# One pipeline, two planners: scheduling the main loop of a two-layer kernel as a block of its own

## The chip, the cores and the metric

The kernel runs on one core of a Trainium2 chip. A core has five engines that each work through their own stream of instructions: TensorE (PE in the profile, with its weight loads as PEld), VectorE (DVE), ScalarE (ACT), GpSimd (POOL) and SyncE (SP), which here only issues DMAs. The streams run beside one another and meet at semaphores. The metric is the device time of one execution in microseconds, the median of three runs.

## The reference

The input is x, 16 sequences of 512 tokens with 256 channels. Two layers are applied, each an attention part and a feed-forward part. Each part first normalises x over the channels, scales and shifts it by values that come from a small condition vector (`mods` in the kernel), and its output is multiplied by a gate from the same condition and added to x.

- Layer 0, attention: q, k and v are projections of the input, passed through a short causal convolution over four tokens and SiLU. Sixteen heads of width 16 then run a recurrence over chunks of 16 tokens. Per head there are two fast weights of 4 x 16, W_in and W_out. For every chunk the softmax of k and of q against W_in over the four rows gives hidden values; they make the output of the chunk and an update of W_out; then W_in and W_out are updated twice by small attentions over the chunk's k and v. A layer norm over each head, an output gate and a projection follow.
- Layer 0, feed-forward: a low-rank network, 256 to 64 to 1024, GELU, back to 64 and to 256.
- Layer 1, attention: sixteen heads, causal, over a window of 64 tokens and the first four tokens of the sequence.
- Layer 1, feed-forward: a channel mix with the token before, `sigmoid(r) * (relu(k)^2 @ W_v)`.

All of it is in 32-bit floating point, apart from masks and some exact helpers in bf16.

## The kernel before

**Units.** The work is cut into 16 units (NU). A unit is 64 tokens (TB) of 8 sequences (HB); the 16 sequences are two halves, and even and odd units belong to the two halves. Layer 0's recurrence carries its state from one unit of a half to the next one of that half, in a bank of PSUM (`fws`).

**Streams.** Five generator functions each do one stage of a unit and yield now and then: `prepare` (normalisation, the projections and convolutions, SiLU at the end of each of q, k and v; results are written to DRAM), `chain` (two pieces of 32 tokens, each two calls of `recur`, the recurrence over 16 tokens, and `finish_piece`), `mlp` (output projection of layer 0's attention, then `low_rank_ffn`), `attend` (`window_attention`) and `mix` (`channel_mix`).

**The order in which it is traced.** `timetable(u)` gives each stream of unit u a number of steps and the times, counted in units, at which they are due: `prepare` from u-1.7, `chain` from u to u+2, `mlp` from u+2, `attend` from u+2.65, `mix` from u+4.1 to u+4.7. The last lines of `adaln_blocks` sort all steps by these times and advance each generator by one step. So instructions of several units and stages are traced interleaved, and the two halves' recurrences run beside each other.

**The order on the engines.** The order of tracing is not the order of issue. The framework takes the traced program with its data dependencies, gives each instruction a priority by its place in the trace, and plays the program through in a simulator: whenever an engine can take an instruction, the ready one of the best priority is put next in that engine's stream. On-chip buffers are assigned at the same time, by what is free in the simulated time. The streams that result are fixed; the chip then executes each in order and waits where the data isn't there. In the kernel before, this simulator is the framework's ordinary core simulator. `tc.high_priority()` raises what is traced under it (the GELU matmuls at line 728 and the bursts of `run`), and `run` (lines 212 to 227) pins a burst of activations that share a table behind one another and then loads the table with Exp and Ln back. The loads that are needed between two activations with different tables are put in afterwards.

**Lines to follow.** In the recurrence: the outer products on POOL (line 526), the scores and sums on DVE (lines 519, 520, 628), the scan on DVE (line 623), exponentials on ACT (line 534). In the window attention: all small matmuls go through one helper at line 865, for scores with queries as rows (`sc`), scores with keys as rows (`st`), scores against the first tokens (`tg`), values (`py`) and sums (`pz`); the masks are added by a matmul at line 862; ACT makes the exponentials `pT` (line 918) and `pg` (line 929) and the reciprocal of the sums `rs` (lines 967, 968); DVE multiplies (`yT`, line 972). In the channel mix: `mix` is made by ACT (line 1021) and DVE (line 1022) in one buffer that is used twice per unit, `pka` (line 1031) is the matmul that reads it, `ka` (line 1043) its relu. Table loads carry lines 217 and 227 where `run` makes them. SP issues every DMA; `load_gate` (line 374) loads a gate into a ring of one buffer per stream.

**Buffers.** PSUM has three rotating banks for projections (`bank`), four for attention scores and the feed-forward (`abank`), and one for the recurrence. The setup ahead of the pipeline (weights, masks, the modulation values and gates) is traced first; its scratch pool is closed before the pools of the pipeline are opened.

Of the kernel before, what the change touches and what calls it, by code (L numbers as in the profile page):

```python
# [95 lines left out]
def adaln_blocks(ctx: ExitStack, tc: tile.TileContext, a: dict, out: bass.AP):  # L96
# [1023 lines left out]
    steps = []  # L1120
    for u in range(NU):
        for n, (f, parts) in enumerate(timetable(u)):
            times = [s + (e - s) * (k + 0.5) / count for count, s, e in parts for k in range(count)]
            stream = f(u)
            steps += [(t, n, k == len(times) - 1, stream) for k, t in enumerate(times)]
    for _, _, last, stream in sorted(steps, key=lambda s: s[:2]):
        next(stream, None)
        if last:
            assert next(stream, steps) is steps


# [52 lines left out]
```

## Time and profile before

| | before |
|---|---|
| median of 3 runs | 3306.56 us (3290.19 to 3310.29) |
| the profiled execution | 3303.97 us, span 3302.2 us |
| granted clock of TensorE, mean | 0.78 |
| busy: PE, DVE | 73%, 73% |
| busy: ACT, POOL | 53%, 51% |
| weight loads of PE | 44% |
| DMA | 186.42 MB, mean 56 GB/s |
| instructions | 46348 |

The profile is one execution. Busy shares are per engine over the span; the forty slices show a digit per fortieth of it (9 is 90% or more); the chain that ended last is followed back from the last instruction, at each step to what released it. Rows of waits name the waiting engine, tile and line, then what released it, then the total, the count and the longest. In rows of the timeline, the bracket is the engine's idle time before the row and its releaser. In the tables of stretches the granted clock is a share of TensorE's full clock.

### The profile page before, as it was taken

What the parts mean: (1) busy time and instruction counts of PE and PEld (TensorE: products, weight loads), DVE (VectorE), ACT (ScalarE), POOL (GpSimd) and SP (SyncE); (2) the same over time, 40 slices, a digit from 0 to 9 for tenths busy, and PEclk for the clock granted to TensorE, in tenths of its full rate; (3) what the DMA queues carried; (4) which work ended last, traced back from release to release, by engine and by line L of the source; (5) the groups of instructions that cost most, each with busy time, mean ns of one, the idle gap of its engine ahead of it and who ended that gap; (6) DMA issues with size and microseconds to landing.
All of it is one profiled execution on the core that took longest, in us unless ns stands there. A gap on an engine that the chain in (4) does not pass through costs nothing.

```text
span 3302.2 us, 46348 instructions
## 1 busy us (share of the span) xinstructions
PE 2424.1 (73%) x16784; PEld 1461.5 (44%) x16784; DVE 2396.2 (73%) x4513; ACT 1762.1 (53%) x3738; POOL 1669.3 (51%) x1575
## 2 busy tenths in 40 slices
PE   3541255777787878788887878788797878878886
PEld 2210123444444445454554445454454455545564
DVE  1678787868887787788778877877878877774221
ACT  1662354556655656565655656565665645444443
POOL 0245555556566655545546555555556556543112
PEclk7675576878787877878778788788878786869887
DMA  5321112032314131231304122131403121212010
GB/s 149 78 62 19 45 40 67 24 72 56 81 33 96 30 83 46 59 78 43 81 21 100 30 70 67 43 88 37 91 17 95 28 71 34 59 35 58 15 29 27
DMA packets 439305, 186.42 MB, mean 56 GB/s; under 512 B 323937, under 2 KB 413090, under 8 KB 439074
## 3 DMA queue, kind: packets, MB, share of 16 engines
q1 hardware_dynamic: 439074, 183.44, 22.8%
q8 instruction: 132, 2.16, 0.3%
q14 instruction: 99, 0.81, 0.1%
HBM read 116.66 MB, written 66.72 MB: 56 GB/s over the span
## 4 chain that ended last, share of the span: by engine, by line
DVE 32%; PE 28%; POOL 18%; ACT 11%; issue 7%; DMA 3%; SPq 1%; POOLq 0%; DVEq 0%; ACTq 0%
POOL pd_o L526 4%; POOL pd_i L526 4%; DVE pd_kv L623 4%; DVE pp L452 3%; DVE sc_v L519 3%; PE ph L728 3%; PE py L865 3%; PE st L865 2%; PE pz L865 2%; DVE sv L520 2%; PE pproj L994 2%; POOL pd_kv L526 2%; DVE mx L881 2%; DVE do L628 2%; PE pka L1031 2%
## 5 line engine op out<-in xcount | busy, mean ns | idle before, releaser
L526 POOL TENSOR_TENSOR pd_o<-e_k,dt_v 128x1024 f32<-128x1024 f32 x128 | 299.0, 2343 | 234.4 <-DVE e_k L541 234.2
L865 PE MATMUL st<-qs,keys 32*128 32x128 f32 x2048 | 234.3, 351 | 107.2 <-DVE mx L881 47.8
L526 POOL TENSOR_TENSOR pd_i<-e_v,dt_k 128x1024 f32<-128x1024 f32 x128 | 297.3, 2354 | 21.4 <-DVE e_v L541 21.1
L865 PEld LDWEIGHTS st<-qs,keys 32*128 32x128 f32 x2048 | 199.5, 240 | 163.0 <-DVE mx L881 61.5
L653 POOL TENSOR_TENSOR pd_kv<-hid,pd_kv 128x1024 f32<-128x1024 f32 x64 | 150.7, 2354 | 188.8 <-DVE fw L624 183.1
L628 DVE TENSOR_REDUCE do<-pd_o 128x64 f32<-128x1024 f32 x126 | 152.5, 1214 | 100.3 <-POOL pd_o L526 100.3
L628 DVE TENSOR_REDUCE di<-pd_i 128x64 f32<-128x1024 f32 x128 | 155.3, 1213 | 85.7 <-POOL pd_i L526 85.7
L865 PE MATMUL sc<-keys,qs 32*128 32x128 f32 x2048 | 169.5, 321 | 63.0 <-DVE mx L881 43.4
L700 PE MATMUL pwo<-w_WoT,oT 128*128 128x256 f32 x256 | 103.1, 560 | 142.6 <-POOL oT L693 140.7
L865 PEld LDWEIGHTS sc<-keys,qs 32*128 32x128 f32 x2048 | 134.6, 210 | 129.8 <-DVE mx L881 63.4
L881 DVE TENSOR_REDUCE mx<-sc 128x4 f32<-128x512 f32 x256 | 168.4, 679 | 19.0 <-PE sc L862 19.0
L623 DVE TENSOR_TENSOR_SCAN pd_kv<-within,pd_kv 128x1024 f32<-128x1024 bf16 x64 | 176.5, 2758 | 1.0
L526 POOL TENSOR_TENSOR pd_kv<-hid,dt_v 128x1024 f32<-128x1024 f32 x64 | 150.1, 2345 | 45.9 <-DVE hid L615 41.0
L519 DVE TENSOR_TENSOR sc_k<-tok,fw 128x1024 f32<-128x1024 f32 x128 | 155.5, 1215 | 16.0 <-ACT tok L589 14.6
L994 PE MATMUL pproj<-w_proj,yT 128*128 128x256 f32 x512 | 136.7, 411 | 36.7 <-DVE yT L972 33.7
L217 ACT ACT_TABLE_LOAD x110 | 141.1, 1283 | 19.7 <-PE pQ L735 18.1
L519 DVE TENSOR_TENSOR sc_v<-tok,fw 128x1024 f32<-128x1024 f32 x128 | 150.4, 1215 | 1.4
L865 PE MATMUL py<-pT,values 128*32 128x128 f32 x2048 | 130.4, 374 | 26.8 <-ACT pT L918 26.3
L520 DVE TENSOR_REDUCE sv<-sc_v 128x64 f32<-128x1024 f32 x128 | 149.7, 1210 | 0.0
L972 DVE TENSOR_TENSOR yT<-py,rs 128x256 f32<-128x256 f32 x128 | 51.5, 415 | 133.8 <-ACT rs L968 133.7
L918 ACT ACTIVATE pT<-st 128x512 f32<-128x512 f32 x256 | 135.4, 615 | 22.0 <-PE st L862 21.8
L865 PE MATMUL py<-pg,vglob 32*32 32x128 f32 x1536 | 71.8, 342 | 99.1 <-ACT pg L929 99.1
(244 smaller groups left out, 6821.5 us busy)
## 6 DMA issues: line engine op xcount, KB each, us to landing
values<-values SPq DMA_DIRECT2D x56, 256.0 KB
gate_a<-gates SPq DMA_DIRECT2D x64, 128.0 KB
xa<-in_x_dram SPq DMA_DIRECT2D x32, 256.0 KB
x<-in_x_dram SPq DMA_DIRECT2D x32, 256.0 KB
gate_c<-gates SPq DMA_DIRECT2D x64, 128.0 KB
gate_d<-gates SPq DMA_DIRECT2D x64, 128.0 KB
q<-y SPq DMA_DIRECT2D x64, 128.0 KB
dt_q<-q SPq DMA_DIRECT2D x32, 256.0 KB
```

Of the source, the lines that this page charges most:

```text
L217: ins = nc.scalar.activation(*args[0], **args[1])
L519: engine.tensor_tensor(pr, tok.unsqueeze(1).to_broadcast(every), w.unsqueeze(2).to_broadcast(every), mul)
L520: nc.vector.tensor_reduce(dst, pr, AX.X, add)
L526: engine.tensor_tensor(pr, hid.unsqueeze(2).to_broadcast(every), tok.unsqueeze(1).to_broadcast(every), mul)
L623: nc.vector.tensor_tensor_scan(flat, within, flat, 0.0, mul, add)
L628: nc.vector.tensor_reduce(t, pr, AX.X, add)
L653: nc.gpsimd.tensor_tensor(po, qh.unsqueeze(2).to_broadcast([P, R, D, CH]), upto, mul)
L700: nc.tensor.matmul(po[:, n * C : (n + 1) * C], lhsT=pair(oT, k, 2 * b2 + n), rhs=w_o[:, k, :], start=k == 0, stop=k == 1,)
L865: nc.tensor.matmul(dst, lhsT=lhsT, rhs=rhs, start=start, stop=False, skip_group_check=True)
L881: nc.vector.tensor_reduce(mx[:, j], sc[j].rearrange("p (s k) -> p s k", s=NS), AX.X, ALU.max)
L918: nc.scalar.activation(pT[j], st[j], AF.Exp)
L994: nc.tensor.matmul(po[:, n * C : (n + 1) * C], lhsT=yT[:, k2, par].rearrange("p e t -> p (e t)"), rhs=w_proj[:, k2, par, :], start=k2 == 0 ...
```

## The change

The loop that advances the generators is put in a `with` block. `tc.block` traces what is inside as a block of its own: it is always entered, and the planner treats it as one piece that is not mixed with what stands outside (here the setup; nothing follows). With `schedule_with_timeline_sim=True` the order inside is made with the framework's timeline model, which keeps track of each engine's sequencer, its execution and its queues apart, in place of the core simulator. The traced instructions, their order of tracing, their engines and their priorities relative to one another stay as they are.

```diff
             stream = f(u)
             steps += [(t, n, k == len(times) - 1, stream) for k, t in enumerate(times)]
-    for _, _, last, stream in sorted(steps, key=lambda s: s[:2]):
-        next(stream, None)
-        if last:
-            assert next(stream, steps) is steps
+    with tc.block(schedule_with_timeline_sim=True):
+        for _, _, last, stream in sorted(steps, key=lambda s: s[:2]):
+            next(stream, None)
+            if last:
+                assert next(stream, steps) is steps
```

## The prediction

> **What bounds the kernel now.** I read the page first: busy shares, the forty slices, the chain that ended last.
>
> ```profile
> span 3302.2 us, 46348 instructions
> PE 2424.1 (73%) x16784; PEld 1461.5 (44%) x16784; DVE 2396.2 (73%) x4513; ACT 1762.1 (53%) x3738; POOL 1669.3 (51%) x1575
> ...
> PE   3541255777787878788887878788797878878886
> ...
> DVE  1678787868887787788778877877878877774221
> ...
> DVE 32%; PE 28%; POOL 18%; ACT 11%; issue 7%; DMA 3%; SPq 1%; POOLq 0%; DVEq 0%; ACTq 0%
> ```
>
> No engine is full, and the chain changes engine all the time: this is a pipeline in which TensorE and VectorE are about equally loaded, and what is lost is lost in hand-overs. So I cut the span into stretches. The scan of line 623 comes back in the chain at 1751.21 and at 2499.59 us, four units apart, so a unit takes 187.1 us in the steady part. The table of stretches has for one such unit, for the end, and (from a second call) for the middle of that unit in steps of 4 us:
>
> ```profile
> 1939.00:2126.00 187.00, 151.98 (x1110) 91.51 (x1106) 150.41 (x280) 110.38 (x234) 102.38 (x98) 0.81 0.24 60
> ...
> 2970.00:3100.00 130.00, 111.45 (x1066) 71.98 (x1066) 47.83 (x103) 66.33 (x137) 43.56 (x54) 0.88 0.16 41
> ...
> 2064.00:2068.00 4.00, 0.00 (x0) 0.00 (x0) 3.93 (x8) 2.70 (x6) 1.89 (x3) 0.85 0.00 0
> 2068.00:2072.00 4.00, 3.94 (x38) 2.17 (x38) 1.88 (x2) 2.98 (x5) 4.00 (x3) 0.50 0.00 0
> 2072.00:2076.00 4.00, 4.00 (x34) 1.51 (x32) 3.83 (x8) 3.10 (x6) 1.36 (x1) 0.50 0.00 0
> 2076.00:2080.00 4.00, 4.00 (x45) 2.32 (x47) 3.86 (x6) 2.83 (x3) 0.00 (x0) 0.50 0.00 0
> 2080.00:2084.00 4.00, 4.00 (x25) 1.32 (x18) 3.65 (x10) 2.49 (x5) 2.95 (x2) 0.94 0.01 4
> ```
>
> Columns: stretch, length, busy time of PE, its weight loads, DVE, ACT and POOL, granted clock, DMA share, GB/s. PE and DVE are busy 152 and 150 of 187 us, so both sit idle for some 35. After PE's stop at 2064 its clock is at half for 12 us. The waits of that unit, and ACT around the stop:
>
> ```profile
> PE py L865 <- ACT pg L929: 11.6, 4, 5.7
> ACT mix L1021 <- PE pka L1031: 9.6, 1, 9.6
> PE st L865 <- ACT rs L967: 5.9, 1, 5.9
> ...
> 2061.78 0.72 ACT L1021 ACTIVATE mix<-hp,mu 128x512 f32<-128x512 f32 x1 [9.62 <-PE pka L1031]
> 2062.40 0.29 ACT L534 ACTIVATE e_v<-e_v 128x128 f32<-128x128 f32 x1
> 2062.60 0.71 ACT L1021 ACTIVATE mix<-hp,mu 128x512 f32<-128x512 f32 x1
> 2063.22 1.54 ACT L918 ACTIVATE pT<-st 128x512 f32<-128x512 f32 x3
> 2066.03 1.09 ACT L1043 ACTIVATE ka<-pka 128x512 f32<-128x512 f32 x2 [1.27 <-DVE mix L1022]
> 2067.00 0.60 ACT L918 ACTIVATE pT<-st 128x512 f32<-128x512 f32 x1
> 2067.63 0.37 ACT L929 ACTIVATE pg<-tg 32x256 f32<-32x256 f32 x1
> ```
>
> This is what an ill-fitting order looks like. PE has the scores for pg ready at about 2063.7 and then stands until 2068.06, because ACT's stream has mix, mix and ka ahead of the fourth pT and of pg, and ka itself waits 1.27 us for DVE. Nothing in the data asks for that order.
>
> **What the Trainium skill says.** "PSUM — Partial Sum Buffer", section "Engine vs sequencer instructions": the queues of ScalarE, VectorE and GpSimd are strict FIFO. The lines above agree: pg waits behind ka though its own input has been there for 4 us. "TensorE: Matmul & The Clock Gate", section "What's actually happening": the clock is at 4/8 or 8/8, set by activity in windows of some 3.4 us. The trace has stretches at 0.50 and at 1.00; the values between fit a switch inside a stretch. So a gap on PE costs more than its length. "ScalarE: Activation LUTs", section "What ACT_TABLE_LOAD costs": 1283 ns for the load, about 2.66 us with a drain. The trace has the 1283; from a load at 2074.15 to the next activation at 2075.44 are 1.29 us, so I use 1.28 without a drain. "Advanced Engine Details and Errata", section "Control Flow Timing": 51 ns for an unconditional branch; this trace has none to compare.
>
> **The change part by part.** No operand, engine or buffer changes. What changes is the model in whose time the planner runs the program while it picks, by priority, what each engine issues next.
>
> *The block's edge.* A branch per engine and a stretch that can't be mixed with the setup. Below: 0, five times 51 ns. Above: one fetch of instructions and a late first transfer; bounded by the setup's own pieces, at most 10 us. The cover is real: the first load of xa is issued at 58.66 us anyway, after the last setup write of gates at 57.02; what starts earlier are memsets and gate loads. I take +3.
>
> *The order on ACT and PE in the steady part.* In one unit PE stands 11.6 us for pg and 5.9 us for rs, 17.5 us, both exponentials or logarithms queued on ACT behind work of other streams. A model that gets PE's and ACT's times nearer to the chip would see pg ready and pick it. Bounds: all of it gone, -17.5; none, 0; below nothing too, because new head-of-queue waits can be made, which I bound at half of the same size, +8.7. I take half gone, -8.7 us a unit: DVE, busy 150 us, then stands at 150/178 = 84%, which is possible. The part at this pace runs from about 600 to 2690 us, 11.2 units: -97 us (ends -196 and +97).
>
> *The clock behind it.* The stop at 2064 was followed by 12 us at half speed, 6 us of lost work. If one such gap in two units goes, that is -3 us a unit, -34 us. Ends: 0, and, were PE never cold (152 x 0.81 = 123 us of work instead of 152), -29 a unit, of which the chain's 28% on PE would take about 8, -90.
>
> *The tables on ACT.* 222 loads in all (110 + 78 + 23 + 8 + 2 + 1 by line); 80 bursts of SiLU, GELU and tanh need 160. The rest are Exps that slip between two GELUs: after 2072.86 the trace has load, e_k, load, GELU, load, e_k, load. The planner's new times move these slips either way; I take 0, and cost the bad case below.
>
> *SP's queue, POOL and DVE.* They are reordered with the rest: SP stands 42.2 us in that unit for one gate load that waits for its only buffer (line 374), with later issues behind it, but DMA is 3% of the chain, so 0, with ±15 for the range. The start (0 to 400 us) and the end (2970 to 3302, PE 82% busy, little else to pick from) have few choices: 0, between -30 and +20.
>
> **Sum:** -97 -34 +3 = -128 us against the profiled execution of 3303.97 us (span 3302.2, 1.8 around it): 3176. The median of the runs, 3306.56, is 2.6 above that execution: 3179, so 3180. What comes late next is DVE.
>
> **The rivals.**
> *Much more (chance 0.07).* Both full ends for waits and clock, -196 -60: about 3050. For: PE's cold time. Against: DVE would be at 150/164 = 91% with its own waits for POOL.
>
> *No difference (0.12).* The two models order alike, or the gaps move to other places because DVE at 80% takes them back. For: idle time on PE and DVE is spread over many short waits (most are below 3 us a unit), so another order may hide these and open others. That the block changes no order at all is in here. Time: 3304 + 3, about 3307.
>
> *Slower by table loads (0.22).* A model whose PE is slower between two GELUs leaves ACT free there, and greedy picking fills the hole with an Exp at 2 x 1.28 us each; loads that are put in later aren't seen by the planner. Seven splits a burst are possible, about two are there now. Five more are 12.8 us a unit, 205 in 16 units, if all lies on the path; PE waits for z (8.6 and 30.3 us on its two rows, over the whole run), so I take half, +103: 3407. It decides once the extra splits cost more than the 128 us gained, from 128/2.57 = 50 on the path, three per burst. For: the slips are there already. Against: PE, ahead of the burst by up to four banks, limits the hole.
>
> **How the numbers follow.** Forecast 0.59, at 3180 with a range of its own from 3080 to 3265; much more 0.07; no difference 0.12; slower 0.22. About 1% (33 us) is what a measurement of this kernel can tell: its three runs spread over 20 us. Faster 0.66, same 0.12, slower 0.22. For 8 in 10 the range runs from 3050 to 3410: it leaves out half of the much faster case and half of the slower one, and the tails of the forecast.
>
> **What would show it.** Right: line 929's pg as releaser of PE's idle time falls from 99.1 us to about half; the scan's period goes from 187 to about 175; PE's clock rises above 0.80 in the middle; table loads stay within 200 to 250. Wrong: pg's waits as before with the same period (no difference), or loads above 300 with more idle time before z and pQ (slower). What I can't see is how well the timeline model knows PE: if it has PE's clock always full, the order of ACT's stream may be as ill-fitting as now.

## The result, and the profile after

The changed kernel takes 3348.98 us (median of four runs, 3339.33 to 3360.08) beside 3304.07 us for the kernel before (four runs). The ratio is 1.014, with an interval from 1.012 to 1.0161: **slower by 45 us**, where the prediction had 3180 us. It lies inside the range, on the wrong side.

The page of the changed kernel: the span, the busy times, the slices of PE and DVE, the chain by engine.

```profile
span 3337.6 us, 46454 instructions
PE 2518.5 (75%) x16784; PEld 1498.8 (45%) x16784; DVE 2427.8 (73%) x4513; ACT 1825.0 (55%) x3788; POOL 1714.4 (51%) x1575
...
PE   3540365868686967788887978878888887889996
...
DVE  1679887877878888888897878597988888621221
...
DVE 37%; PE 28%; ACT 15%; POOL 8%; issue 6%; DMA 5%; SPq 1%; POOLq 0%; DVEq 0%; ACTq 0%
```

Two things stand out. PE has the same 16784 instructions and is busy 2518.5 us with them, before 2424.1. And DVE's last slices are emptier while PE's are fuller: work that PE used to do beside DVE is left for the end. The rows of one line show the same: the scan of line 623 (the recurrence) and the last multiplication of the channel mix, line 1077, each with its first and last start. First the kernel before, then the changed one:

```profile
L623 DVE TENSOR_TENSOR_SCAN pd_kv<-within,pd_kv x64: 2257/2292/4425, 128.1 to 2974.8; 128x1024 f32<-128x1024 bf16 x64
...
L1077 POOL TENSOR_TENSOR sg<-sg,gate_d x32: 1262/1268/1281, 799.5 to 3294.0; 128x512 f32<-128x512 f32 x32
```

```profile
L623 DVE TENSOR_TENSOR_SCAN pd_kv<-within,pd_kv x64: 2248/2292/4432, 139.7 to 2876.1; 128x1024 f32<-128x1024 bf16 x64
...
L1077 POOL TENSOR_TENSOR sg<-sg,gate_d x32: 1262/1269/3287, 801.3 to 3329.3; 128x512 f32<-128x512 f32 x32
```

The recurrence ends 98.7 us earlier (2974.8 to 2876.1); the pipeline ends 35.3 us later. The stretch from the last scan to the last `sg` grew from 319.2 to 453.2 us. The table of stretches, first the middle of the kernel before, then the middle, one unit and a part of the end of the changed kernel (columns as in the prediction):

```profile
1187.00:2690.00 1503.00, 1219.82 (x8832) 741.64 (x8833) 1212.14 (x2252) 878.43 (x1859) 825.35 (x767) 0.80 0.25 59
```

```profile
1187.00:2690.00 1503.00, 1233.29 (x8246) 740.66 (x8239) 1249.85 (x2299) 886.77 (x1859) 882.16 (x761) 0.77 0.24 59
...
1939.00:2126.00 187.00, 143.45 (x995) 87.91 (x993) 146.33 (x276) 105.06 (x219) 108.66 (x98) 0.73 0.25 62
...
2970.00:3100.00 130.00, 119.03 (x1039) 74.27 (x1037) 28.08 (x71) 62.71 (x128) 24.18 (x44) 0.86 0.16 41
```

In the same 1503 us DVE gets more done (2299 instructions instead of 2252), and PE gets 8246 matmuls done instead of 8832 although it is busy longer. The mix of matmuls in the two windows isn't quite the same, but PE doesn't wait more: it is busy longer with what it does. Its clock there is 0.77, before 0.80. The waits that the prediction named, over the whole run of the changed kernel (columns: who waits for whom, total, count, longest):

```profile
PE py L865 <- ACT pg L929: 77.9, 35, 8.6
...
PE ph L728 <- ACT z L217: 29.2, 11, 7.9
...
PE st L865 <- ACT rs L967: 7.9, 2, 4.4
```

The wait for `pg` went from 99.1 to 77.9 us, the one for `rs` from 36.1 to 7.9; the one for `z` rose from 8.6 to 29.2. PE's idle time in the middle is 1503 minus busy: 283 before, 270 after. Over the whole span it fell by 59 us (878.1 to 819.1) while PE's busy time rose by 94.4, and the difference is the 35.4 us by which the profiled spans differ. So the new order did take waits from PE; it lost more than that in PE's own time.

The two stages show it too. Eight units apart, the scan starts at 1183.1 and 2677.5 us before and at 1186.1 and 2595.4 after: a unit takes 186.8 us before and 176.2 after. The `sg` of the channel mix starts at 1167.4 and 2662.9 before and at 1171.8 and 2759.2 after: 186.9 and 198.4 us a unit. The recurrence got faster and the last stage slower.

**Where PE's time went.** If each stretch of PE's busy time is put down to the instruction that extends it, the first GELU matmul `ph` takes 50 us more than before (116.0 to 166.5), `sc` 43 (236.1 to 279.0) and `pQ` 39 (86.4 to 125.2); all others together take 38 less. All three use a part of the array: `ph` reads 64 rows (even and odd f lie on the two halves, line 728), `pQ` writes 64 columns, `sc` reads 32 rows. This is PE's timeline in a stretch of the feed-forward, of the kernel before and of the changed one (columns: start, length of the whole row, what, how many instructions; a 32-bit matmul is two):

```profile
1707.57 1.12 PE L728 MATMUL ph<-PT,w_v 64*128 64x512 f32 x2
1708.62 0.55 PE L354 MATMUL pt_a<-blocks,xn_a 128*128 128x128 f32 x3
1709.00 1.03 PE L1051 MATMUL pr<-w_W_rT,mix 128*128 128x256 f32 x4
1709.96 1.13 PE L728 MATMUL ph<-PT,w_v 64*128 64x512 f32 x4
```

```profile
1703.62 1.08 PE L865 MATMUL py<-pT,values 128*32 128x128 f32 x16
1704.63 2.07 PE L728 MATMUL ph<-PT,w_v 64*128 64x512 f32 x2
1706.63 0.64 PE L865 MATMUL py<-pT,values 128*32 128x128 f32 x4
1707.20 2.07 PE L728 MATMUL ph<-PT,w_v 64*128 64x512 f32 x2
```

The first fence is the key to the whole result. At 1707.57 one `ph` alone takes 1.12 us; at 1709.96 two of them, next to one another, take 1.13. **A pair on the two halves of the array costs as much as one.** In the changed kernel the same matmuls stand singly between `py` and `pz`, and at half clock: 2.07 us each. The rest of its trace agrees. A `ph` that stands alone adds 1.05 us to PE's busy time at full clock and 2.01 at half (means of 20 and 44 of them), a pair 1.11 and 2.01 (6 and 11). In the middle, 69% of the `ph` instructions start at half clock, before 44%. In PE's stream the planner's order has 92 separate runs of `ph` where the kernel before has 69, for 64 pairs. The Trainium skill, "TensorE: Matmul & The Clock Gate", section "Part 3: Packing small matmuls — row/col tiling", says that matmuls on different tiles of the array overlap and that matmuls start and end in the order of the program. The rows agree with the overlap, two in 1.13 us, and none of them is out of order. Together the two mean that the neighbours of a matmul in PE's stream decide whether the overlap can happen.

**Where ACT's time went.** There are 272 table loads instead of 222. Of the 50 more, 38 are at other lines than those of `run` and 534, above all at the Lns and Exps of lines 196, 197, 967 and 968. ACT's timeline in one GELU burst of the changed kernel:

```profile
2107.22 0.69 ACT L217 ACTIVATE z<-ph,c_b 128x512 f32<-128x512 f32 x1
...
2108.22 1.28 ACT L196 ACT_TABLE_LOAD   x1
2109.51 0.23 ACT L196 ACTIVATE ov<-ov 128x32 f32<-128x32 f32 x1
2109.76 1.28 ACT L202 ACT_TABLE_LOAD   x1
2111.05 0.26 ACT L202 ACTIVATE lrt<-lrt 128x64 f32<-128x64 f32 x1
2111.33 1.28 ACT L196 ACT_TABLE_LOAD   x1
...
2119.20 0.69 ACT L217 ACTIVATE z<-ph,c_b 128x512 f32<-128x512 f32 x1
```

Between these two GELUs stand seven loads, six of them for activations that take under 2 us together: lines 196 and 203 take a Ln, 197 and 202 an Exp, the chains of two streams alternate, and each change is a load. The Trainium skill, "ScalarE: Activation LUTs", section "Table sets: the hidden batching unit", names a set that has both Ln and Exp, so that one load serves both. The trace agrees where `run` has loaded that set itself (line 227): 165 Lns and 689 Exps run on such loads and on none of their own. After the loads that are put in afterwards it differs: there, 26 Lns and 62 Exps, no Exp runs on a load that was put in for a Ln, nor a Ln on one for an Exp. Which set such a load brings, the trace doesn't tell. A burst of eight GELUs takes 27.7 us on average from the first to the last, before 16.8, with 262 other activations and copies in all bursts together instead of 99.

### The profile page after: what moved, and what is told of

It reads as the page before. It is cut to its first block, busy times and chain, and to the rows that moved or that the text cites. A ratio compares the mean times of both kernels' runs of the same rounds, so it can differ in the third digit from the quotient of the medians.

```text
span 3337.6 us, 46454 instructions
## 1 busy us (share of the span) xinstructions
PE 2518.5 (75%) x16784; PEld 1498.8 (45%) x16784; DVE 2427.8 (73%) x4513; ACT 1825.0 (55%) x3788; POOL 1714.4 (51%) x1575
## 4 chain that ended last, share of the span: by engine, by line
DVE 37%; PE 28%; ACT 15%; POOL 8%; issue 6%; DMA 5%; SPq 1%; POOLq 0%; DVEq 0%; ACTq 0%
DVE pd_kv L623 4%; DVE pp L452 3%; PE sc L865 3%; DVE sv L520 3%; DVE sc_v L519 3%; DVE di L628 3%; DVE sc_k L519 2%; PE py L865 2%; POOL pd_o L526 2%; DVE scs L520 2%; PE st L865 2%; PE pproj L994 2%; DVE mx L881 2%; PE ph L728 2%; PE pz L865 2%
## 5 line engine op out<-in xcount | busy, mean ns | idle before, releaser
L700 PE MATMUL pwo<-w_WoT,oT 128*128 128x256 f32 x256 | 91.3, 521 | 209.4 <-POOL oT L693 209.4
L865 PEld LDWEIGHTS sc<-keys,qs 32*128 32x128 f32 x2048 | 174.6, 205 | 122.2 <-issue 83.2
L865 PE MATMUL sc<-keys,qs 32*128 32x128 f32 x2048 | 214.4, 315 | 19.3 <-DVE mx L881 17.8
L728 PE MATMUL ph<-PT,w_v 64*128 64x512 f32 x256 | 172.3, 916 | 33.9 <-ACT z L217 29.2
L526 POOL TENSOR_TENSOR pd_kv<-hid,dt_v 128x1024 f32<-128x1024 f32 x64 | 173.9, 2717 | 7.3 <-DVE hid L615 4.2
L700 PEld LDWEIGHTS pwo<-w_WoT,oT 128*128 128x128 f32 x256 | 66.4, 272 | 225.9 <-POOL oT L693 212.4
L382 POOL TENSOR_TENSOR x<-x,up_c 128x512 f32<-128x512 f32 x32 | 44.5, 1391 | 236.6 <-DVE up_c L380 236.6
```

The source lines that it names most:

```text
L526: engine.tensor_tensor(pr, hid.unsqueeze(2).to_broadcast(every), tok.unsqueeze(1).to_broadcast(every), mul)
L700: nc.tensor.matmul(po[:, n * C : (n + 1) * C], lhsT=pair(oT, k, 2 * b2 + n), rhs=w_o[:, k, :], start=k == 0, stop=k == 1,)
L728: nc.tensor.matmul(ph, lhsT=w_v1[rows, f // 2, :], rhs=pT[rows], start=True, stop=True)
L865: nc.tensor.matmul(dst, lhsT=lhsT, rhs=rhs, start=start, stop=False, skip_group_check=True)
```

## The experiments

The ratios are to the kernel before, run beside each on the same chip, with 95% intervals. Medians of different rows can come from different chips.

| run | what | median us | ratio |
|---|---|---|---|
| e1_block | block without the timeline model | 3301.45 | 1.0008 [0.9996, 1.0019] |
| e2_lock | recurrence held back | 3396.93 | 1.0289 [1.0267, 1.031] |
| e3_dve | DVE held to the old order | 3474.77 | 1.0525 [1.0504, 1.0545] |
| e4_pe | PE held to the old order | 3325.0 | 1.0069 [1.0048, 1.0089] |
| e5_revpe | old plan, PE held to the new order | 3450.06 | 1.0465 [1.0436, 1.0494] |
| e9_peact | PE and ACT held to the old order | 3263.54 | 0.9894 [0.987, 0.9917] |
| e10_act | ACT held to the old order | 3468.3 | 1.052 [1.0498, 1.0542] |
| e7_notab | changed kernel without tables | 3251.54 | 0.986 [0.9837, 0.9882] |
| e8_notab0 | kernel before without tables | 3282.46 | 0.9958 [0.9929, 0.9987] |
| e11_group | changed, GELUs in threes | 3359.1 | 1.0173 [1.014, 1.0205] |
| e12_group0 | before, GELUs in threes | 3334.14 | 1.0118 [1.0069, 1.0168] |
| e13_grpin | e11_group, PE held to the old order | 3351.99 | 1.0169 [1.0134, 1.0205] |
| e17_cutph | before, `ph` pairs cut | 3343.88 | 1.0129 [1.0107, 1.0152] |
| e18_ph | changed, `ph` pairs together | 3322.12 | 1.0066 [1.0043, 1.0089] |
| e19_peactph | e9_peact, `ph` pairs together | 3259.84 | 0.9865 [0.9845, 0.9884] |
| e20_notabph | e7_notab, `ph` pairs together | 3220.58 | 0.975 [0.9725, 0.9774] |
| e21_loads | before, 51 more table loads | 3328.52 | 1.0084 [1.0064, 1.0105] |

### The block's edge

```diff
-    with tc.block(schedule_with_timeline_sim=True):
+    with tc.block():
```

> The block alone, planned by the core simulator: the planned streams are those of the kernel before but for ten neighbours on DVE, POOL and SP. Theory run-ahead (the recurrence is issued ahead of the stages that feed PE, and PE's missing work comes back at the end): ratio to before 0.998 to 1.004, the loss is all in the order. Rival edge of the block (branches, fetch, separation from the setup): 1.01 or more.

1.0008, with 1 in the interval. Entering a block costs nothing that can be told from noise, and with the core simulator the order stays as it was but for a few neighbours. The 45 us are the timeline model's.

### First theory: the recurrence runs ahead

In DVE's stream the recurrence's instructions stand earlier and earlier, by some 72 places on average in the last quarter, and all else stands later. The trace has the last scan 99 us early. So the first theory was that the run-ahead starves the later stages. e2_lock makes the first score of `recur` wait, in the order of issue alone, for a piece of the window attention of an earlier unit; e3_dve gives DVE the whole order of the kernel before. To hold an engine to an order, the program is planned twice: the first plan yields the order, the second gets it as a rule.

```diff
+        first = scores(half, nc.vector, k, w_in, sc[:, :, :CH], f"k{tag}")
+        at = (u - 4 + pc, c)
+        if at in gated:
+            tc.add_manual_dep(first.ins, gated[at].ins.name, mybir.DependencyInfo(mybir.DependencyClass.NoSync, mybir.DependencyReason.DATA), reason="in step")
...
-            gated_residual("c", x, b2, po, gt, f"c{i}_{b2}")
+            gated[i, b2] = gated_residual("c", x, b2, po, gt, f"c{i}_{b2}")
```

> The timeline plan, with an issue-order edge on DVE that keeps each recurrence step behind an earlier unit's attention output; in the planned DVE stream the recurrence is then at most half a unit ahead of where it was before, against a whole unit in the changed kernel. Run-ahead: about half of the loss is gone, ratio to before 1.000 to 1.009, and the time from the last scan to the end falls from 461 us to 360 to 420. Rival table loads (272 instead of 222, 64 us of ACT) or rival local order on PE: no change from the hold, 1.012 to 1.018.

```diff
+        here = {i.name: i for i in nc.cur_bb.bb.instructions}
+        for names in order:
+            names = [n for n in names if n in here]
+            for one, two in zip(names, names[1:]):
+                tc.add_manual_dep(here[two], one, mybir.DependencyInfo(mybir.DependencyClass.NoSync, mybir.DependencyReason.DATA), reason="pinned")
...
+    engines = [getattr(mybir.EngineType, e) for e in ['DVE']]
```

> The timeline plan with DVE's stream pinned to the order that the core simulator makes; PE, ACT, POOL and SP are planned by the timeline model around it. Run-ahead: ratio 0.985 to 1.004, last scan within 15 us of before's 2975, tail about 320 us. Rival local order on PE: 1.012 to 1.018, since PE's stream still differs in half of its places. Rival table loads: goes with the number of loads in the trace, 1.3 us each on ACT.

1.0289 and 1.0525, both above every range that was expected. Without the run-ahead (last scan at 3012.4 and 3144.2 us) the kernel is slower still, and PE's busy time rises further, to 2547.6 us in e2_lock and 2629.1 in e3_dve. As the rest is planned anew around a hold, these two runs alone wouldn't settle it. Later ones do: the scan ends at 2846.9 us in e4_pe and at 2790.2 in e20_notabph, earlier than in the changed kernel, and both are faster than it. **The theory falls**, and PE's busy time pointed to PE.

### Second theory: PE's order

The same rule, with PE's order in place of DVE's (e4_pe), with PE's and ACT's (e9_peact), with ACT's alone (e10_act); and the reverse, the old plan around PE's new order (e5_revpe).

```diff
-    engines = [getattr(mybir.EngineType, e) for e in ['DVE']]
+    engines = [getattr(mybir.EngineType, e) for e in ['PE']]
```

> The timeline plan with PE's stream pinned to the order of the core simulator; DVE, ACT, POOL and SP planned by the timeline model, the recurrence still runs ahead on DVE. Run-ahead: ratio 1.010 to 1.025, tail from the last scan above 430 us. Rival local order on PE: 0.995 to 1.004, and the clock in the middle back at 0.80.

```diff
-    planned = program(False, ())
+    planned = program(True, ())
...
-    nc = program(True, order)
+    nc = program(False, order)
```

> The reverse of the pinned PE: the core simulator plans ACT, DVE, POOL and SP around PE's stream as the timeline model made it. Theory PE's stream (runs of matmuls on parts of the array are cut up, so they overlap less and PE's own time grows): ratio to before 1.006 to 1.016, PE's time for sc about 275 us instead of 236 and for ph above 140 instead of 116. Theory bursts (GELUs on ACT split by Exps and table loads hold up ph and pQ): loads stay near 222, ratio 0.997 to 1.004. Theory run-ahead, which two runs speak against: 0.997 to 1.004 too.

```diff
-    engines = [getattr(mybir.EngineType, e) for e in ['PE']]
+    engines = [getattr(mybir.EngineType, e) for e in ['PE', 'Activation']]
```

> The timeline plan with the streams of PE and ACT both pinned to the order of the core simulator; only DVE, POOL and SP are planned by the timeline model. PE's stream and bursts together: PE's busy time back at 2420 us, 222 loads, ratio 0.990 to 1.003. If the rest of the timeline plan costs by itself: 1.005 or more.

```diff
-    engines = [getattr(mybir.EngineType, e) for e in ['PE', 'Activation']]
+    engines = [getattr(mybir.EngineType, e) for e in ['Activation']]
```

> The timeline plan with ACT's stream alone pinned to the core simulator's order (222 loads, 69 of them inside GELU bursts, as before); PE's stream is the timeline model's. Theory slips (Exps planned into the holes of a GELU burst bring loads that the planner doesn't see, and stretch the burst from 17 to 28 us): ratio 0.990 to 1.004. Theory PE's stream (the timeline model's order on PE is what costs): 1.010 or more.

With PE's order from before, half of the loss is gone (1.0069); with PE's new order in the old plan it is three times as large (1.0465). The first lies between the ranges that were expected, the second above all of them. The sharpest pair is e9_peact and e10_act, which differ only in whether PE is held: 3263.54 and 3468.3 us, 205 us apart. Their busy times, e9_peact first:

```profile
PE 2363.5 (72%) x16784; PEld 1435.1 (44%) x16784; DVE 2425.2 (74%) x4513; ACT 1754.9 (54%) x3738; POOL 1702.3 (52%) x1575
```

```profile
PE 2589.2 (75%) x16784; PEld 1562.6 (45%) x16784; DVE 2434.3 (70%) x4513; ACT 1762.6 (51%) x3738; POOL 1708.1 (49%) x1575
```

Only PE's busy time differs by much, by 226 us for the same instructions. e9_peact, in which the timeline model orders DVE, POOL and SP alone, is 1.06% faster than the kernel before. These runs exchange the whole stream, so they show the engine, not yet the cause. And PE's stream in e10_act isn't that of the changed kernel: it was planned anew around ACT's old order and has 107 runs of `ph`, so 205 us is more than the change's own order on PE costs.

One more pair is in these runs. e4_pe and e9_peact have the same order on PE and differ in whether ACT is held: some 60 us (1.0069 and 0.9894). PE's busy time differs by 55 us (2418.4 and 2363.5), nearly all of it in two tiles: `pQ` takes 119.4 and 86.6 us, `ph` 135.5 and 115.2. **ACT's order costs PE time even where PE's own order is the old one.** In e4_pe the GELU bursts take 23.5 us, in e9_peact 17.0. That a pair doesn't overlap when what its second matmul needs comes late, although the two are neighbours, would fit; it isn't shown by itself.

### Third theory: the table loads

e7_notab and e8_notab0 replace SiLU, GELU and tanh by Identity, in the changed kernel and in the one before, and leave out the loads back; the functions are left out of the computation, and no table is switched in the pipeline. Both programs are planned anew without them.

```diff
-            burst.append(((z, ph, AF.Gelu_apprx_tanh), dict(bias=b1[:, f : f + 1])))
+            burst.append(((z, ph, AF.Identity), dict(bias=b1[:, f : f + 1])))
...
-            back = nc.scalar.preload_act_table_set("natural_log_exp_and_others")
-            tc.keep_in_program_order(back)
```

> The changed kernel with SiLU, GELU and tanh of the bursts replaced by Identity, and without the loads that bring Exp and Ln back: nearly no table loads are left, and the output is not the reference's. Bursts: faster than its twin with the core simulator's plan or equal to it, 0.985 to 1.003 of the twin, and pQ and ph on PE back at 86 and 116 us. PE's stream: still 1.007 to 1.016 of the twin, pQ and ph as in the changed kernel.

> The twin: the kernel before with the same functions replaced and the same loads left out. Both theories: 0.95 to 0.99 of before, 222 loads of 1.28 us are gone from ACT and part of them was waited for.

The order turns round: without tables the changed kernel is the faster one, 3251.54 against 3282.46 us. With tables and with the plan that goes with them, the changed kernel takes 97.4 us more, the kernel before 21.6. Neither theory had it whole. The ratio is the one of the bursts, but `ph` and `pQ` stayed at 151.0 and 115.7 us, where it had them back at 116 and 86; and the twin gained less (0.9958) than the 0.95 to 0.99 expected. Fewer loads are then the thing to try: GELUs that become ready in threes leave fewer holes (e11_group; e12_group0 is the same in the kernel before, e13_grpin with PE held).

```diff
-        run(burst, [evac])
+        run(burst, [phs[2]], {3: [phs[5]], 6: [phs[7]]})
```

> The changed kernel with GELUs let go in threes: the first of each three waits for the third's matmul, so the planner sees no hole between them. 217 loads in the planned stream instead of 272, 84 instead of 125 inside the bursts. Slips: ratio to before 0.996 to 1.008, so better than the changed kernel's 1.014 by 0.6% or more. PE's stream: 1.010 to 1.020.

> The same threes in the kernel before: 203 loads instead of 222, 46 inside the bursts instead of 69. Slips: 0.990 to 1.003, a small gain at most, since its bursts take 17 us with or without loads. PE's stream: no difference, 0.998 to 1.005.

> Threes, timeline plan, and PE pinned to the core simulator's order of the kernel with threes: 200 loads, 39 inside the bursts, the recurrence still ahead on DVE. Slips and PE's stream together: 0.975 to 0.995, against 1.007 for the pinned PE with 260 loads. If only PE's stream mattered: 1.003 to 1.010, as with the pinned PE alone.

The loads fall to 217, 203 and 200, and none of the three is faster than its own kernel without threes (1.0118 and 1.0169 lie above every range for e12_group0 and e13_grpin). Waiting for a third `ph` evidently costs more than the loads it saves. As a remedy this failed. The threes bring changed and before nearer to one another (3359.1 and 3334.14, 25 us instead of 45), with 14 loads between them instead of 50, but their intervals overlap, so this is weak evidence.

### One cause at a time

e17_cutph keeps the whole order of the kernel before and only puts the second matmul of a `ph` pair up to four places later in PE's stream; e18_ph keeps the timeline plan and puts the pairs together; e19_peactph does that in e9_peact.

```diff
+        for k in range(len(names) - 2, -1, -1):
+            one, two = names[k : k + 2]
+            g = groups.get(one)
+            if g and g[1] in ('ph',) and groups.get(two) == g:
+                after = k + 2
+                while after < k + 4 + 2 and names[after] not in groups:
+                    after += 1
+                names.insert(after - 1, names.pop(k + 1))
```

> The order of the kernel before, in which of the 64 pairs of ph matmuls (two matmuls of 64 rows each, on the two halves of the array) the second is put up to four places later, behind instructions of other tiles, so that the pair no longer stands together (93 runs of ph in PE's stream instead of 69); DVE, ACT and POOL keep their order but for nine neighbours. Theory (cut runs cost PE its overlap): a cut pair takes about 1.0 us more at full clock and 2.0 at half clock, so PE's time on ph goes from 116 us to between 145 and 175, and the time rises by a fifth to all of that, ratio 1.003 to 1.016. Rival (ph grew in the changed kernel through the clock or through waits, not through its neighbours): ph between 112 and 126 us, ratio 0.998 to 1.002.

```diff
+            held.setdefault(g, []).append(n)
+            if last[g] == k:
+                out += held.pop(g)
```

> The order of the timeline plan, in which the ph matmuls of a pair are put together again (57 runs of ph instead of 92); the other engines are planned around it and move by one to two places. Theory (cut runs): ph goes from 166 us to between 100 and 130, and the time falls from the changed kernel's ratio of 1.014 to between 0.998 and 1.010. Rival (the cause lies elsewhere, in the other engines' order or the table loads): ph stays above 145 us, or falls and the ratio stays between 1.011 and 1.018.

> The plan with PE and ACT held to the order of the kernel before (0.989), with the few ph pairs that are apart in it put together as well (60 runs of ph instead of 69, 54 of pQ instead of 62). Theory (cut runs): ph 115 to about 105 us, ratio 0.983 to 0.989. Rival (adjacency no longer matters once most pairs stand together, or other orders matter more): 0.988 to 0.993.

The row of `ph` (busy us, mean ns) in the kernel before, the changed kernel, e17_cutph and e18_ph, in that order:

```profile
L728 PE MATMUL ph<-PT,w_v 64*128 64x512 f32 x256 | 120.3, 831 | 16.5 <-ACT z L217 8.6 <-ACT PT L718 7.8
```

```profile
L728 PE MATMUL ph<-PT,w_v 64*128 64x512 f32 x256 | 172.3, 916 | 33.9 <-ACT z L217 29.2
```

```profile
L728 PE MATMUL ph<-PT,w_v 64*128 64x512 f32 x256 | 164.4, 845 | 12.4 <-ACT PT L718 7.8
```

```profile
L728 PE MATMUL ph<-PT,w_v 64*128 64x512 f32 x256 | 114.9, 881 | 24.1 <-ACT z L217 17.4 <-DVE yT L976 3.4 <-ACT rs L971 2.9
```

And e17_cutph's busy times:

```profile
PE 2465.8 (74%) x16784; PEld 1466.5 (44%) x16784; DVE 2395.6 (72%) x4513; ACT 1766.1 (53%) x3738; POOL 1669.7 (50%) x1575
```

**Cutting 24 more runs, with all else nearly as before, costs 41 us** (3343.88 against 3302.61, the kernel before beside it), and PE's busy time rises by the same 42 (2424.1 to 2465.8): 1.7 us for each run that is cut, between the 1.12 us of a single at full clock and the 2.07 at half. PE's clock in the middle is 0.80 as before, so a lower mean clock is not the reason. Putting the pairs together in the changed kernel takes 27 us off (3348.98 to 3322.12). The three runs came in where the theory of cut runs expected them. So cut `ph` pairs are a cause by themselves, of 27 us in the changed kernel and 41 in the old order.

`sc` and `pQ` take 43 and 39 us more of PE's time in the changed kernel, and no run puts those together again. `sc` follows PE's order: in e4_pe it is back at 236.1 us. `pQ` doesn't: in e4_pe it stands in the same 62 runs as before, where the changed kernel has 90, and still takes 119.4 us. e19_peactph, at 0.9865, is the fastest of the kernels that leave nothing out: 43 us below the kernel before.

### What the order gives, and what the loads take

e20_notabph is e7_notab with PE's pairs put together as in e18_ph; e21_loads adds loads to the kernel before.

```diff
+    nc = program(True, [together(n) for n in order])
```

> The timeline plan without tables (SiLU, GELU and tanh replaced by Identity and the loads back left out, as in e7_notab; those functions are left out of the computation), with the ph matmuls of a pair put together. Theory (the change is a sum of three: a gain by the order, a loss by cut ph pairs, a loss by extra table loads): with both losses taken out the gain stands alone, 27 to 42 us below e7_notab, ratio 0.973 to 0.979. Rival (cut pairs cost time only where the loads have made PE late): as e7_notab, 0.983 to 0.988.

```diff
+                if k in split:
+                    tc.keep_in_program_order(nc.scalar.preload_act_table_set("natural_log_exp_and_others"))
...
-        run(burst, [evac])
+        run(burst, [evac], (0, 6))
```

> The order of the kernel before with a load of the Exp table after the first and the seventh GELU of each unit, so that the table of GELU has to be loaded again: 273 loads in place of 222, about as many as the changed kernel has (272). 51 loads of 1.28 us are 65 us of ACT; a few runs of ph and pQ are cut by it too (75 runs of ph for 69, 76 of pQ for 62), up to 15 us. Theory (loads inside a burst are on the path): 25 to 80 us, ratio 1.008 to 1.024. Rival (ACT is busy half of the time and hides them): 0.999 to 1.005.

Both came in where the sum of three expected them, e21_loads at the lower edge. The changes of the median, against the twin that differs in that point:

| term | from | us |
|---|---|---|
| the order by itself | e20_notabph - e8_notab0 | -61.9 |
| cut `ph` pairs | e7_notab - e20_notabph | +31.0 |
| tables, above what they cost before | (after - e7_notab) - (before - e8_notab0) = 97.4 - 21.6 | +75.8 |
| sum | | +44.9 |

The sum closes because the terms are differences in a ring; what supports it is that the terms have been seen elsewhere: the pairs at +41 and -27. By the ratios, each to the kernel before beside it, the terms are -69, +36 and +79. The first and the last are less sure than that, for the plans without tables are other plans. In e8_notab0 `ph` stands in 52 runs, as in e20_notabph (53), but takes 144.0 us where e20_notabph has 103.2 and the kernel before 116.0; 133 of its 256 instructions are at half clock, before 102. Had it stayed at 116.0, the order's gain and the tables' loss would both be smaller by up to 28 us (an estimate from these busy times).

The tables are only partly explained. 51 more loads in the kernel before cost 27 us, some of it for a few runs that the new order cuts. The changed kernel has about as many more loads and loses 76. Its loads stand in bursts of 27.7 us, those of e21_loads in bursts of 18.6. The pair e4_pe and e9_peact puts some 60 us on ACT's order, with 38 more loads, and finds them again as PE's time on `pQ` and `ph`; but it exchanges the whole stream of ACT and doesn't part the loads from the other work in the bursts. **About 50 us of the tables' row, or some 20 if the 28 above belong elsewhere, stay open.** Also open is why PE takes 61 us less in e9_peact than before with the same order.

## Why the prediction was wrong

**The block's edge, +3: not contradicted.** e1_block has +2.6 us by its ratio, in an interval from -1 to +6.

**The order in the steady part, -97: the step that failed, and half of it was right.** The waits for `rs` shrank by more than half, those for `pg` by a fifth; together they fell by 49 us over the run. The sign that was named came: the scan's period went from 187 to 176 us, where about 175 was forecast. That the last scan is 98.7 us early, nearly the 97, is in part luck, as the two waits gave only half of it. What failed is the step from a wait that goes, and the scan that comes round sooner, to "a unit takes less". The prediction read the period of the whole pipeline from the scan in the chain. In a pipeline with buffers the scan can run ahead; the stages that live on PE didn't follow, the channel mix came every 198 us instead of 187, and its work was left for the end. The end, put at 0, between -30 and +20, is 134 us longer if it is counted from the last scan.

The deeper fault is in the same step: it let the order move waits and left PE's own 152 us of a unit untouched. PE's idle time fell by 59 us over the run, but its busy time rose by 94 for the same 16784 matmuls, which no term of the sum was for. Part of it is that a plan decides which matmuls are neighbours, and with parts of the array that changes how long the same instructions take: e18_ph gets 42 us of PE's busy time and 27 us of the run back by that alone. PE's rows of the kernel before have a single `ph` and a pair at 1.12 and 1.13 us, so this could be seen ahead.

**The clock, -34: wrong sign.** It was to rise above 0.80 in the middle and fell to 0.77. The waits that it was tied to did become fewer. But the middle has as many stretches at half clock as before, 69 and 70, and they are longer: 689 us in all instead of 592, with PE busy for 86 and 85% of them. By an estimate from these figures that is some 43 us of PE's work at full clock. It is no fourth term, since the terms above were measured at the clock that each run had; why the stretches are longer stays open, as no run holds the clock apart. The sum of the much faster rival also takes 60 us for the clock's full end where its own part has 90.

**The tables, 0: wrong, and the rival priced them by their count alone.** 272 loads lie between the marks that were set (200 to 250, above 300). The slower rival needed about 50 extra splits, some 100 loads, on the path to cancel the gain; there were 50 loads. Its mechanism is part of the answer: Exps, and above all Lns, fill the holes between GELUs and aren't seen by the planner. But 50 loads at 1.28 us are 64 us on ACT, and the loss by tables is 76: there was more to it than the count. The rival alone, without cut pairs, would have missed the one cause that runs isolate in both directions.

**SP, POOL and DVE, 0:** not undone one by one. With their new order and PE's and ACT's old one the kernel is 36 us faster than before (e9_peact), so together they were worth a gain, not nothing. **What comes late next, DVE:** its share of the chain rose from 32 to 37%, as expected, but the last slices of the span are PE's.

## What to carry to other kernels

Before an order is changed, look in PE's timeline for matmuls that use a part of the array and compare a single one with a pair: if the two take the same time, their being neighbours is worth as much as the instruction, and a planner that doesn't know it can spend it. Split the result into the engine's idle and its busy time: an order can change both. The pace of one stage in the chain isn't the pace of the pipeline; compare the last start of every stage. And a planner that doesn't see table loads is a risk on the engine that switches tables: in this kernel, holding PE and ACT to their old order, with the pairs together, and letting the model plan the rest turned +1.4% into -1.35%.

## What the runs showed of the hardware

- Two 64-row 32-bit matmuls of 512 columns on the two halves of the array take 1.13 us together when they are neighbours and 1.12 us each when something stands between; at half clock a single one takes 2.07 us.
- PE ran at half clock also where it had matmuls without a pause: at 2072 to 2080 us of the kernel before it is busy 8.00 of 8 us at a granted clock of 0.50, after it had stood still from 2064 to 2068. In the middle of the changed kernel 69% of the `ph` instructions start at half clock.
- The same matmuls in the same order on PE can take longer when ACT's order changes: `pQ` 119.4 us in e4_pe and 86.6 in e9_peact, in 62 runs each.
- On ACT, a Ln and an Exp in turn cost a load of 1.28 us at each change when no load of line 227 stands ahead of them since the last GELU: six such loads between two GELUs at 2108 to 2118 us of the changed kernel.
